# Starting the tiles of the normalized x at multiples of 64 bytes of a partition

## The chip, the core and the metric

The kernel runs on one core of one Trainium2 chip. The metric is the time of one execution on the device in microseconds. The kernel before takes 344.67 us, the median of three runs (344.66 to 345.06).

## What is computed

A block of a transformer with two residual steps, for 2 sequences of 512 tokens with 1,024 features each. First, the layer-normalized x and a context are rounded to 8 bits, centred and multiplied; the product is added to x. Then the sum is layer-normalized again and goes through a shared gated MLP (512 hidden columns) and, for each token, two routed experts (256 hidden columns each).

```python
x = x + tanh(g_xattn[0]) * matmul(fake_quant(layernorm(x)), fake_quant(ctx))
xt = layernorm(x)                                  # 1024 tokens x 1024
gate = router(xt)                                  # 2 of 16 experts for a token
for w1, b1, w2, b2, w3, b3, ge in experts:
    h = silu(xt @ w1 + b1) * (xt @ w2 + b2)        # 256 hidden columns
    y = y + ge[:, None] * (h @ w3 + b3)
z = silu(xt @ sw1 + sb1) * (xt @ sw2 + sb2) @ sw3 + sb3    # 512 hidden columns
x = x + tanh(g_ffn[0]) * (y + z)
```

With these inputs only two experts are chosen by any token, so the kernel computes two experts for all 1,024 tokens and weights them by the gates. More experts, or unusual zero points, lead to branches that are not taken here.

## The kernel before

Tokens are handled in 8 tiles of 128 rows, X0 to X7, four for each sequence (batch) b. All float32 products of the MLPs are made from two pieces of each operand, a high part[...] and the low rest: high x high, high x low and low x high, three passes over 8 blocks of 128 features.

The second normalization's result is transposed on TensorE (`px`, L288) and split into a high tile XH and a low tile XL for each batch. `xh` (L145, mostly on ScalarE) copies the high part out of PSUM; `xl` (L298, VectorE) writes the rest. Each of the four tiles is 128 partitions x 8 blocks x 512 tokens of float32, 16,384 bytes of a partition. They are the moving operand of every up-projection, with the weights (in slabs) as the stationary one:

- L476 (`um`) and L327 (`up_mm`), 256 tokens wide: the first units of the shared MLP, 288 and 96 matmuls.
- L327 (`up_mm`), 512 tokens wide: the rest of the shared MLP (192 matmuls in bank tiles named sp), expert 0 (192, e0p) and expert 1 (192, e1p).

GpSimd also adds XH and XL to one float32 tile xf for the router (L557). In the down-projections (`down`, L372, L373, L375, and `down_last`, L360 to L362, for the last tile) the hidden values are the stationary operand, and the moving one is a slab of weights, 512 columns wide (256 in the last two pieces of the last tile): 192 matmuls for the shared MLP, 96 for expert 0, and 84 + 6 of 512 columns and 12 of 256 for expert 1. The names are spo, e0po and e1po for the outputs, sd, e0d and e1d for the weights, sh, e0h and e1h for the hidden values; h or l at the end is the high or low part.

The tiles of batch 1 share their places with the attention. Slot `xh1` first holds qT of each batch in turn (the quantized x, transposed, bf16, stationary) and then XH1; slot `xl1` first holds cq (the quantized context, bf16, moving) and then XL1. The attention's matmuls are at L233.

The first part, up to about 95 us, is a list of steps written out by hand (START); behind it the program's order holds. All loads and stores are started by SyncE's queue.

SBUF is laid out by pools, in the order in which they are opened: const, keep, small, route, slabs (22 buffers of 4,096 bytes). A slot begins at a multiple of 32 bytes. In the built program of the kernel before, the tiles begin at these bytes of a partition:

| tile or pool | first byte | modulo 64 |
|---|---|---|
| X0 to X7, 4,096 each (pool keep) | 21664 | 32 |
| XH0 | 54432 | 32 |
| XL0 | 70816 | 32 |
| slot xh1: qT, then XH1 | 87200 | 32 |
| slot xl1: cq, then XL1 | 103584 | 32 |
| pool small | 119968 | 32 |
| first slab | 138240 | 0 |
| end of the last slab | 228352 | 0 |

Every block of XH or XL is 2,048 bytes long and every slab 4,096, so all blocks of a tile have the tile's place modulo 64.[...]

Of the kernel before, what the change touches and what calls it, by code (L numbers as in the profile page):

```python
# [10 lines left out]
F32R = mybir.dt.float32r  # L11
BF16 = mybir.dt.bfloat16
# [6 lines left out]
P = 128  # L19
D = 1024  # L20
KD = D // P
B = 2
S = 512
TB = S // P
# [7 lines left out]
SC = 2 * INTER // P  # L32
EPS = 1e-5
LOWEST = -3.4028234663852886e38

# the order in which the start's loads and steps are issued, each step as function.arguments
LOADS = "x.1 x.3 c.0 c.1 x.2 c.2 c.3 c.4 c.5 c.6 c.7.0 c.7.1 w.1.1 x.4 b w.1.0 w.0.1 x.5 w.0.0"
# [40 lines left out]
def flamingo_block(  # L78
# [5 lines left out]
    of = out.rearrange("b s d -> (b s) d")  # L84

    const = ctx.enter_context(tc.tile_pool(name="const", bufs=1))
    keep = ctx.enter_context(tc.tile_pool(name="keep", bufs=1))
# [14 lines left out]

# [1 line left out]
    sc_in = const.tile([P, 6], F32, name="sc_in")  # L104
    nc.sync.dma_start(sc_in, scal.partition_broadcast(P))

# [1 line left out]
    X = [keep.tile([P, D], F32, name=f"X{t}") for t in range(NT)]  # L108

    # the engine that starts the DMAs; the paths that are rarely taken use GpSimd's queue  # L110
    dq = [nc.sync]
# [5 lines left out]

# [1 line left out]
    mhalf = const.tile([P, 1], F32, name="mhalf")  # L119
# [12 lines left out]
    nc.vector.tensor_scalar(nz, sc_in[:, 0:4], -1.0, None, ALU.mult)  # L132
    # zero points that bf16 holds exactly, less any quantized value, are integers of 0..255
    z8 = const.tile([P, 4], U8, name="z8")
# [20 lines left out]
    H = D // 2  # L155
    half = lambda h: ts(h, H)
# [3 lines left out]

# [1 line left out]
    def bn(t, h):  # L162
# [8 lines left out]
    def qa(t, eng):  # L171
        rb = [small.tile([P, 1], F32, name=f"{n}{t}", tag=n, bufs=4) for n in ("r", "qa", "qb")]
        ab_[t] = rb
        pick(eng).tensor_scalar(rb[0], mv_[t][:, 1:2], EPS, None, ALU.add)

# [36 lines left out]

# [1 line left out]
    c8_, raws, qT, cq, acc = {}, {}, {}, {}, {}  # L214
# [21 lines left out]

# [1 line left out]
    sq_, md_, xn_, px_ = {}, {}, {}, {}  # L238

    def e(t, h):  # L240
        """The residual and its sum."""
        if h == 0:
            sq_[t] = [small.tile([P, 2], F32, name=f"{n}{t}", tag=n, bufs=4) for n in "sq"]
        xs = X[t][:, half(h)]
        nc.vector.scalar_tensor_tensor(  # L245
            xs, acc[t][h], cx_scale, xs, ALU.mult, ALU.add, accum_out=sq_[t][0][:, h : h + 1]
        )

    def sq(t, h):
        """H^2 times the squared deviations from the mean of half a row, H values."""  # L250
        if h == 0:
            xn_[t] = slab(f"xn{t}", F32)
        s, q = sq_[t]
        nc.scalar.activation(  # L254
            xn_[t][:, half(h)], X[t][:, half(h)], AF.Square,
            bias=s[:, h : h + 1], scale=-float(H), accum_out=q[:, h : h + 1],
        )

    def fm(t, eng):
        """The mean, and what the difference of the halves' means adds to the variance."""  # L260
        s, eng = sq_[t][0], pick(eng)
        d = small.tile([P, 1], F32, name=f"d{t}", tag="d", bufs=4)
        eng.tensor_tensor(d, s[:, 0:1], s[:, 1:2], ALU.subtract)
        eng.tensor_scalar(d, d, d, H / 2.0, ALU.mult, ALU.mult)
        nm = small.tile([P, 1], F32, name=f"nm{t}", tag="nm", bufs=4)
        eng.tensor_scalar(nm, s[:, 0:1], s[:, 1:2], -1.0 / D, ALU.add, ALU.mult)
        md_[t] = nm, d

    def fc(t, eng):
        d = md_[t][1]  # L270
        pick(eng).tensor_scalar(d, sq_[t][1][:, 0:1], d, EPS * D * H * H, ALU.add, ALU.add)

# [33 lines left out]

# [1 line left out]
    def load_up(name, w1, w2, c):  # L308
# [44 lines left out]
    def down_last(name, t, hid, w3, scale):  # L353
        """A tile in column pieces, each stored as soon as it is done."""
        n = len(hid)
        for lo, w in ((0, 512), (512, 256), (768, 256)):
            cols = slice(lo, lo + w)
            po = bank(f"{name}po{t}_{lo}")[:, :w]
            for c, ((hh, hl), (wh, wl)) in enumerate(zip(hid, w3)):
                nc.tensor.matmul(po, hh[:, ts(t, P)], wh[:, cols], start=c == 0, stop=False)  # L360
                nc.tensor.matmul(po, hh[:, ts(t, P)], wl[:, cols], start=False, stop=False)
                nc.tensor.matmul(po, hl[:, ts(t, P)], wh[:, cols], start=False, stop=c == n - 1)  # L362
            nc.vector.scalar_tensor_tensor(X[t][:, cols], po, scale, X[t][:, cols], ALU.mult, ALU.add)
            dq[0].dma_start(of[ts(t, P), cols], X[t][:, cols])
# [22 lines left out]

    # ================= program =================
    XH, XL = ([keep.tile([P, KD, S], F32R, name=n), None] for n in ("XH0", "XL0"))
    sw1c = lambda c: sw1[:, ts(c, P)].rearrange("(k p) n -> p k n", p=P)  # L390
# [21 lines left out]
    for load in LOADS.split():  # L412
        kind, *at = load.split(".")
        at = [int(a) for a in at]
# [15 lines left out]

# [1 line left out]
    bT = const.tile([P, NB], F32, name="bT")  # L432
# [5 lines left out]

    # TensorE's clock is low until it has been busy for a few microseconds
    zero = const.tile([P, S], BF16, name="zero")  # L440
# [8 lines left out]

    # biases of the hidden layers, as columns  # L450
    def pb():
# [5 lines left out]

    # shared weights, split: half h of the rows of matrix i, hidden columns c
    def wh(c, i, h, eng):
# [8 lines left out]

    # hidden columns c of tokens lo..lo+255: matrix i, pass p of three
    def um(c, lo, i, p):  # L470
# [38 lines left out]

    # router weights, padded to the columns of a quarter of TensorE, and constants of the router  # L510
    rwf = const.tile([P, KD, QC], F32, name="rwf")
# [5 lines left out]
    lowest = const.tile([P, NT * E], F32, name="lowest")  # L517
# [9 lines left out]
    def stage(b):  # L527
        """The buffers of a batch's attention."""
        qT[b] = keep.tile([P, TB, KD, P], BF16, name=f"qT{b}", tag="xh1")
        cq[b] = keep.tile([P, KD, D], BF16, name=f"cq{b}", tag="xl1")  # L530

    def xx():
        XH[1], XL[1] = (keep.tile([P, KD, S], F32R, name=n, tag=n.lower()) for n in ("XH1", "XL1"))

# [8 lines left out]

# [1 line left out]
    def rt(name, shape=(P, NT, E), dtype=F32):  # L545
# [6 lines left out]
    def router_x(b):  # L552
        """The normalized x, transposed, in one float32 piece."""
        xs = []
        for i in range(4):
            x = slab(f"xf{b}_{i}", F32, (P, 2, S))
            nc.gpsimd.tensor_tensor(  # L557
                x, XH[b][:, ts(i, 2)].bitcast(F32), XL[b][:, ts(i, 2)].bitcast(F32), ALU.add
            )
            xs.append(x)  # L560
        return xs

    # the four quarters of TensorE's columns work at the same time, each on a fourth of the rows of D
    def router_logits(b, lT, xs):
# [19 lines left out]
    def first_max(name, v, n):  # L584
        """One-hot of the first largest of the last n."""
        m = rt(f"{name}m", (P, NT))
        nc.vector.tensor_reduce(m, v, AX.X, ALU.max)
        o = rt(f"{name}o", (P, NT, n))
        nc.vector.tensor_tensor(o, v, over(m, n), ALU.is_equal)
        order = tie[:, E - n :].unsqueeze(1).to_broadcast([P, NT, n])  # L590
        nc.vector.tensor_mul(o, o, order)
        nc.vector.tensor_reduce(m, o, AX.X, ALU.max)
        nc.vector.tensor_tensor(o, order, over(m, n), ALU.is_equal)
        return o

    # of all experts some token chose: 16 - e; of the others: 0
    key = route.tile([P, E], F32, name="key")
# [48 lines left out]
    def next_expert(j):  # L646
        """Of the chosen experts left, the one of lowest index: its index, gates and hidden biases."""
        m = rt(f"m{j}", (P, 1))
# [19 lines left out]

# [1 line left out]
    def expert(j, e, gv, bv, store):  # L670
# [32 lines left out]

    # the rest of the shared MLP's hidden layer, with the router in between
    lT = slab("lT", F32)
# [17 lines left out]
    chosen = [next_expert(j) for j in range(2)]  # L723
# [3 lines left out]

# [1 line left out]
    def attention_exact(b):  # L729
# [64 lines left out]

# [1 line left out]
    n_exp = nc.values_load(n_chosen[0:1, 0:1], min_val=2, max_val=E)  # L796
# [54 lines left out]
```

## Time and profile before

| | |
|---|---|
| median of three timed runs | 344.67 us |
| span of the profiled execution, first to last instruction | 342.9 us |
| what the timed median has beyond that span | 1.8 us |
| TensorE matmuls | busy 321.7 us, 94% of the span |
| VectorE / ScalarE / GpSimd | busy 57% / 28% / 23% |
| TensorE's granted clock, mean | 0.989 |
| DMA traffic | 31.45 MB, mean 92 GB/s |

The profile gives the profiled execution's time as its span; what the device adds before the first and after the last instruction is the third row, taken from the timed runs. A matmul's duration in the profile contains its way through the array, which overlaps with the next one's. How many matmuls fit into a stretch of time is read from their starts, and that pace is what counts in a stream of them.

### The profile page before, as it was taken

The page shows a single profiled execution, that of the slowest core. Times are in us where ns is not written, and L with a number is a line of the kernel's source. Part 1 is how long each engine was busy: PE and PEld are TensorE (multiplying, and loading weights), DVE is VectorE, ACT ScalarE, POOL GpSimd, SP SyncE. Part 2 cuts the span into 40 slices and gives each one's busy share as a digit, 9 for nine tenths or more (in the row PEclk, how much of TensorE's full clock was granted, in tenths as well). Part 3 has the DMA queues.
Part 4 walks back from the last instruction along what each step waited for, and adds up shares of the span by engine and source line. Part 5 has one row for each costly group of instructions (what it writes and reads, how often), then busy time and mean ns, then how long its engine had stood idle before and what let it go on. Part 6 is the DMA issues. An engine that isn't in the chain of part 4 may idle for free.

```text
span 342.9 us, 4322 instructions
## 1 busy us (share of the span) xinstructions
PE 321.7 (94%) x1673; PEld 254.5 (74%) x1673; DVE 197.0 (57%) x335; ACT 95.4 (28%) x148; POOL 79.0 (23%) x110
## 2 busy tenths in 40 slices
PE   6588899989999999999999999999999999999990
PEld 2244886769998686888888888888888888888870
DVE  3879999879723126736754632494484135834560
ACT  2756877672213135120200002112400012030000
POOL 2795798868600740000000000000000000000000
PEclk9899999999999999999999999999999999999997
DMA  6999920000004033101200091201310400001542
GB/s 207 420 375 391 399 62 0 2 0 2 0 2 123 9 118 122 63 0 59 66 0 0 8 329 33 62 2 32 90 61 2 122 0 2 0 0 50 198 183 74
DMA packets 25892, 31.45 MB, mean 92 GB/s; under 512 B 2492, under 2 KB 19204, under 8 KB 25860
## 3 DMA queue, kind: packets, MB, share of 16 engines
q1 hardware_dynamic: 25860, 31.05, 26.5%
q8 instruction: 17, 0.28, 0.3%
q14 instruction: 15, 0.12, 0.1%
HBM read 26.85 MB, written 4.19 MB: 91 GB/s over the span
## 4 chain that ended last, share of the span: by engine, by line
PE 75%; DVE 8%; POOL 5%; ACT 4%; issue 3%; DMA 2%; SPq 0%; DVEq 0%; POOLq 0%
PE sp L327 16%; PE e1p L327 13%; PE e0p L327 13%; PE sp L476 5%; PE spo L373 4%; PE spo L372 4%; PE spo L375 4%; ACT xn L254 2%; PE e0po L372 2%; PE e0po L373 2%; PE e0po L375 2%; PE e1po L373 2%; PE e1po L372 2%; PE e1po L375 2%; DVE xn L283 2%
## 5 line engine op out<-in xcount | busy, mean ns | idle before, releaser
L233 PE MATMUL at<-cq,qT 128*128 128x512 bf16 x128 | 30.3, 379 | 2.5 <-POOL cq L153 1.5
L557 POOL TENSOR_TENSOR xf<-XH,XL 128x1024 f32<-128x1024 f32 x8 | 19.9, 2497 | 22.4 <-PE sp L327 19.6
L233 PEld LDWEIGHTS <-qT 128*128 128x128 bf16 x128 | 12.1, 98 | 15.5 <-issue 2.9
L378 DVE SCALAR_TENSOR_TENSOR X<-spo,tg,X 128x512 f32<-128x512 f32 x16 | 11.3, 746 | 16.0 <-PE spo L375 16.0
L338 DVE SCALAR_TENSOR_TENSOR ssa<-sp,bT,ssa 128x512 f32<-128x512 f32 (+1 forms) x6 | 4.0, 662 | 26.1 <-PE sp L327 26.1
L337 ACT ACTIVATE e0sa<-e0p,bv 128x512 f32<-128x512 f32 x4 | 2.8, 690 | 49.4 <-PE e0p L327 49.4
L378 DVE SCALAR_TENSOR_TENSOR X<-e0po,gv,X 128x512 f32<-128x512 f32 x16 | 11.3, 747 | 7.3 <-PE e0po L375 7.3
L283 DVE TENSOR_SCALAR xn<-X,nm,d 128x512 f32<-128x512 f32 x16 | 13.8, 891 | 1.4 <-POOL d L279 1.3
L378 DVE SCALAR_TENSOR_TENSOR X<-e1po,gv,X 128x512 f32<-128x512 f32 x14 | 9.9, 747 | 8.2 <-PE e1po L375 8.2
L288 PE MATMUL px<-ident,xn 128*128 128x128 f32 x64 | 9.3, 275 | 3.5 <-DVE xn L283 2.3
L337 ACT ACTIVATE e1sa<-e1p,bv 128x512 f32<-128x512 f32 x4 | 2.8, 690 | 34.9 <-PE e1p L327 34.9
L338 DVE SCALAR_TENSOR_TENSOR e1sa<-e1p,bv,e1sa 128x512 f32<-128x512 f32 x4 | 3.0, 752 | 15.9 <-PE e1p L327 15.9
L254 ACT ACTIVATE xn<-X,s 128x512 f32<-128x512 f32 x16 | 11.4, 716 | 1.9 <-DVE X L245 1.4
L245 DVE SCALAR_TENSOR_TENSOR X<-at,cx_scale,X 128x512 f32<-128x512 f32 x16 | 11.6, 742 | 0.1
L165 DVE BATCH_NORM_STATS2 st<-X 128x6 f32<-128x512 f32 x16 | 10.3, 680 | 2.2 <-DMA X<-in_dram 2.2
L338 DVE SCALAR_TENSOR_TENSOR e0sa<-e0p,bv,e0sa 128x512 f32<-128x512 f32 x4 | 3.0, 751 | 14.6 <-PE e0p L327 14.6
L288 PEld LDWEIGHTS px<-ident,xn 128*128 128x128 f32 x64 | 7.2, 141 | 5.6 <-ACT XH L145 2.6
L298 DVE TENSOR_TENSOR XL<-px,XH 128x512 fp32r<-128x512 f32 x16 | 10.4, 679 | 0.8 <-ACT XH L145 0.8
L386 DVE SCALAR_TENSOR_TENSOR X<-sbias,tg,X 128x1024 f32<-128x1024 f32 x8 | 10.3, 1284 | 0.3
L153 POOL TENSOR_SCALAR cq<-q8c,nz 128x1024 bf16<-128x1024 uint8 (+1 forms) x8 | 10.0, 1250 | 1.0 <-DVE q8c L223 0.6
L208 PE MATMUL pq<-ident_b,qx 128*128 128x128 bf16 x64 | 5.4, 228 | 4.7 <-ACT qx L151 4.4
L386 DVE SCALAR_TENSOR_TENSOR X<-e1bias,gv,X 128x1024 f32<-128x1024 f32 x8 | 9.8, 1280 | 0.0
(402 smaller groups left out, 830.9 us busy)
## 6 DMA issues: line engine op xcount, KB each, us to landing
cr<-in_dram SPq DMA_DIRECT2D x15, 512.0 KB, 9.2
out_dram<-X SPq DMA_DIRECT2D x15, 256.0 KB, 2.4
X<-in_dram SPq DMA_DIRECT2D x7, 512.0 KB, 9.0
X<-in_dram SPq DMA_DIRECT2D x2, 256.0 KB, 4.1
cr<-in_dram SPq DMA_DIRECT2D x2, 256.0 KB, 9.1
sb1r<-in_dram SPq DMA_DIRECT2D x1, 512.0 KB, 9.0
sa1r<-in_dram SPq DMA_DIRECT2D x1, 512.0 KB, 7.2
sb0r<-in_dram SPq DMA_DIRECT2D x1, 512.0 KB, 8.2
```

Source lines behind the costliest of these rows:

```text
L233: nc.tensor.matmul(acc[t][h], qT[b][:, t % TB, k, :], cq[b][:, k, half(h)], start=(k == 0), stop=(k == KD - 1))
L254: nc.scalar.activation(xn_[t][:, half(h)], X[t][:, half(h)], AF.Square, bias=s[:, h : h + 1], scale=-float(H), accum_out=q[:, h : h + 1],)
L283: nc.vector.tensor_scalar(xn_[t][:, half(h)], X[t][:, half(h)], nm, r, ALU.add, ALU.mult)
L288: nc.tensor.transpose(px_[t, q][:, k, :], xn_[t][:, ts(4 * q + k, P)], ident)
L327: nc.tensor.matmul(p, wx[:, k, :], xx[b][:, k, cols], start=first and k == 0, stop=last and k == KD - 1)
L372: nc.tensor.matmul(po[h], hh[:, ts(t, P)], wh[:, ts(h, 512)], start=first, stop=False)
L373: nc.tensor.matmul(po[h], hh[:, ts(t, P)], wl[:, ts(h, 512)], start=False, stop=False)
L375: nc.tensor.matmul(po[h], hl[:, ts(t, P)], wh[:, ts(h, 512)], start=False, stop=last)
L378: nc.vector.scalar_tensor_tensor(xs, po[h], scale, xs, ALU.mult, ALU.add)
L386: nc.vector.scalar_tensor_tensor(X[t], bb, scale, X[t], ALU.mult, ALU.add)
L476: nc.tensor.matmul(up_[c, lo, i], w[:, k, :], x[0][:, k, lo : lo + 256], start=p == 0 and k == 0, stop=p == 2 and k == KD - 1,)
L557: nc.gpsimd.tensor_tensor(x, XH[b][:, ts(i, 2)].bitcast(F32), XL[b][:, ts(i, 2)].bitcast(F32), ALU.add)
```

## The change

The four tiles XH0, XL0, XH1 and XL1, and qT and cq that share slots with the latter two, are asked for with an alignment of 64 bytes. All tiles of one slot ask for the same. Comments and docstrings go too, and two empty lines take the place of comments; no instruction is added, removed or put elsewhere.

```diff
 EPS = 1e-5
+
+LINE = 64
 LOWEST = -3.4028234663852886e38
...
-    XH, XL = ([keep.tile([P, KD, S], F32R, name=n), None] for n in ("XH0", "XL0"))
+    XH, XL = ([keep.tile([P, KD, S], F32R, name=n, align_bytes=LINE), None] for n in ("XH0", "XL0"))
...
     def stage(b):
-        """The buffers of a batch's attention."""
-        qT[b] = keep.tile([P, TB, KD, P], BF16, name=f"qT{b}", tag="xh1")
-        cq[b] = keep.tile([P, KD, D], BF16, name=f"cq{b}", tag="xl1")
+
+        qT[b] = keep.tile([P, TB, KD, P], BF16, name=f"qT{b}", tag="xh1", align_bytes=LINE)
+        cq[b] = keep.tile([P, KD, D], BF16, name=f"cq{b}", tag="xl1", align_bytes=LINE)
 
     def xx():
-        XH[1], XL[1] = (keep.tile([P, KD, S], F32R, name=n, tag=n.lower()) for n in ("XH1", "XL1"))
+        XH[1], XL[1] = (keep.tile([P, KD, S], F32R, name=n, tag=n.lower(), align_bytes=LINE) for n in ("XH1", "XL1"))
```

By the tile library's description, a pool that is asked for an alignment begins the slots of that tag on it wherever the pool's base is, and reserves the alignment less 32 bytes for each such tag. With four tags that is 4 x 32 = 128 bytes. Worked out from the table above: X0 to X7 stay; XH0 begins at 54464, XL0 at 70848, slot xh1 at 87296, slot xl1 at 103680, all multiples of 64; the pool small begins at 120096 and the first slab at 138368, each 128 further and at the same place modulo 64.

## The prediction, made before the change was run

> **What bounds the kernel now.** I read the page first (section 1, then the chain), then the groups by form on TensorE, then the chain in order of time, and last the timeline where a pace can be read from starts.
>
> ```profile
> span 342.9 us, 4322 instructions
> PE 321.7 (94%) x1673; PEld 254.5 (74%) x1673; DVE 197.0 (57%) x335; ACT 95.4 (28%) x148; POOL 79.0 (23%) x110
> PE 75%; DVE 8%; POOL 5%; ACT 4%; issue 3%; DMA 2%; SPq 0%; DVEq 0%; POOLq 0%
> ```
>
> TensorE is busy for 94% of the span and is 75% of the chain that ended last. Busy is not yet bound, so the chain's order matters more:
>
> ```profile
> 95.05 22.64 PE sp L327 x144
> 117.68 1.85 PE pl L568 x16
> 119.54 11.44 PE sp L327 x48
> 130.98 1.85 PE pl L568 x16
> 132.83 0.59 PE plt L578 x4
> 133.42 0.47 PE sp L327 x2
> 134.33 22.02 PE sp L327 x94
> ...
> 200.13 44.98 PE e0p L327 x192
> 245.10 0.23 PE e0po L372
> ...
> 266.87 44.98 PE e1p L327 x192
> 311.85 0.23 PE e1po L372
> ```
>
> From 95 us to about 333.7 us nothing but matmuls stands on the chain. In that stretch a nanosecond per matmul is a nanosecond of the kernel, times their number. The paces follow from the starts: an up-projection stage of an expert is 44.98 us for 192 matmuls, 234.3 ns each. The down-projection between them, from 245.10 to 266.87, is 21.77 us for 96 (eight tiles of 12), 226.8 ns each. Both stream 512 float32 columns and load 128x128 float32 weights before each one. Their durations show the same step:
>
> ```profile
> L373 PE MATMUL e0po<-e0d0l,e0h0h 128*128 128x512 f32 x16 | 6.2, 389 | 0.0
> L327 PE MATMUL e0p<-XH,e0a0h 128*128 128x512 f32 x16 | 4.1, 396 | 0.0
> L327 PE MATMUL e0p<-XL,e0b1h 128*128 128x512 f32 x16 | 4.1, 396 | 0.0
> ```
>
> Every 512-wide group that streams XH or XL stands at 396 or 397 ns apart from two that begin a stage (407 and 409); every one that streams a slab (sd, e0d, e1d) stands at 389 or 390 (395 for the first of all). By the memory map of the kernel before, XH and XL begin 32 bytes past a multiple of 64 and the slabs begin on one. That is the one fact that lines up with the change.
>
> **The change part by part.**
>
> *Addresses.* Nothing is removed, added or moved in any engine's order or in SP's or POOL's queue; there is no new wait. Only addresses differ: XH0, XL0 and the two shared slots go from 32 to 0 modulo 64. What lies behind `keep` moves too. The pool reserves 32 bytes for each of the four aligned tags, 128 in all, so `small`, `route` and the slabs move by 128 and keep their place modulo 64. It still fits: the slabs end at 228,480 of 229,376 bytes.
>
> *512-wide up-projections.* They are 192 in the shared MLP (48 for c=1, 48 for c=2, 96 for c=3) and 192 in each expert: 576. The nearest row for "the same matmul from a tile on a multiple of 64" is the down-projection, 226.8 ns. 576 x (234.3 - 226.8) = 4.3 us, all on the chain. Bounds: nothing, if the 7.5 ns has another cause; and 576 x (234.3 - 217) = 10 us, if alignment also took away what the float32 stream pays over the bf16 one. That stream is in the trace too:
>
> ```profile
> 69.63 1.03 PE L233 MATMUL at<-cq,qT 128*128 128x512 bf16 x4
> ```
>
> Four matmuls take 1.03 us including the last one's 379 ns, so three starts are 0.65 us apart, 217 ns each. I take 226.8, because the slabs have the alignment and still stand there. Here the Trainium skill speaks twice. TensorE: Matmul & The Clock Gate, section "Back-to-back issue gap", has N/2.4 + 2.5 ns, 215.8 at N = 512, and its account of a matmul's steps says that weights come over a read port of their own and take nothing from the stream. The bf16 row agrees; the float32 rows, at 226.8 and 234.3 with a weight load beside each, do not. By the rule the sum would be 576 x 18.5 = 10.7 us; by the rows it is 4.3, and I follow the rows. SBUF — State Buffer, section "Specifications (TRN2)", speaks against the change: its cachelines have 16 bytes. A tile 32 bytes past a multiple of 64 starts on such a line already, and 2,048 bytes of a row cover 128 lines either way. By that rule the change is worth nothing and the time stays at 344.7. The two paces stand against it, but they don't show that the address is what parts them; that is the largest doubt here, and it is rival 1.
>
> *256-wide up-projections.* 288 at L476 and 96 at L327. Their pace is 0.95 us for 8 in the rows below, 119 ns; the nearest aligned row is the end of the last tile, whose starts at 332.33, 332.45 and 332.57 are 120 ns apart.
>
> ```profile
> 94.88 1.11 PE L327 MATMUL sp<-XH,sa0h 128*128 128x256 f32 x8
> 95.83 1.11 PE L327 MATMUL sp<-XL,sa0h 128*128 128x256 f32 x8
> ...
> 332.33 0.28 PE L362 MATMUL e1po<-e1d0h,e1h0l 128*128 128x256 f32 x1
> 332.45 0.28 PE L360 MATMUL e1po<-e1d1h,e1h1h 128*128 128x256 f32 x1
> 332.57 0.28 PE L361 MATMUL e1po<-e1d1l,e1h1h 128*128 128x256 f32 x1
> ```
>
> So here alignment buys nothing, and may cost 1.2 ns each: 0.5 us if all 384 were on the chain. About 230 are (all 96 at L327, and at L476 17% of the chain's first 95 us, some 135), so I take 0.3 us. Bounds: 0.5 us lost; or 0.7 us gained, if they came to 116 ns, the lowest spacing among them (230 x 3 ns).
>
> *Attention and other engines.* cq lies off 64 before, and its bf16 stream already runs at 217 ns: nothing. The writes of XH and XL (L145, L298) and POOL's sum of the two (L557, 2497 ns each) keep their sizes. In the first 95 us some writes are on the chain ("DVE XL L298" is 3.4% of it, 3.2 us). No row shows an aligned twin, so 5% either way is 0.2 us, and I take zero. POOL's sums run beside matmuls; if that cover were gone, 5% of 19.9 us is 1 us.
>
> *What is late next.* With up-projections 3% shorter, the weights of the following stage must still be split in time. The timeline has the low part of e1's first down weights made by DVE from 303.10 for 1.23 us, used from 311.9; e0a1's low part ends at 215.1, used at 226.2. Each is ready 7 us or more ahead, against 1.4 us that a stage loses, and their own releases move forward with TensorE. The routing result that pcn (L637) waits for is ready at 146.8, 9 us ahead. Nothing takes the place of the time saved. The tail behind the last matmul (add, store, 9.2 us) is unchanged.
>
> *Sum.* -4.3 + 0.3 = -4.0 us against the profiled execution's span of 342.9 us: 338.9. The median of the timed runs, 344.67, stands 1.8 us above that span; what lies around it does not change, so 344.67 - 4.0 = 340.6 us. By its own bounds this case runs from 339.7 (4.3 and 0.7 gained) to 340.9 (4.3 gained, 0.5 lost), and with 0.2 us for the writes from 339.5 to 341.1.
>
> **The rivals.**
>
> *1. Another cause, or a larger boundary; no change.* Up and down streams differ in more than the address: up takes a new stationary tile for each matmul where down loads one for several, and up writes 24 times into one bank where down alternates. Against the bank: the last tile's 512-wide pieces (L360 to L362) write one bank six times in a row at 227 ns. Against the weights: the step between two hidden blocks in the down stream changes them at no extra time. And slabs are at multiples of 1,024, so the rows can't say that 64 is enough. The 256-wide rows, with no gain from alignment, speak for this rival. Time: 344.7, within 0.5. It also covers a request that moves no tile.
>
> *2. The boundary is 128 bytes; half the gain.* By the arithmetic of the map XH0 and XL0 land 64 past a multiple of 128, and XH1 and XL1 on one. Then only batch 1 speeds up: 48 + 48 + 48 + 96 + 96 = 336 matmuls x 7.5 = 2.5 us, so 342.2.
>
> *3. The slabs go off 64; slower.* If the pool grew by 32 bytes and not 128, every slab would begin 32 past a multiple of 64: the weights of all up-projections, and both operands of the down ones. If a matmul is slow as soon as either operand is off, up stays at 234.3 and the 378 + 6 512-wide down-projections rise from 226.8 to it: 2.9 us, 347.5. It decides from the point where the reserve is an odd multiple of 32 and the weights' place counts; if only the stream's place counts, this layout still gains 4.3 - 2.9 = 1.4 us. Against it stands the pool's own description, 32 per tag.
>
> **How the numbers follow.** The forecast has 0.66, rival 1 0.16, rival 2 0.09, rival 3 0.09. About 0.2% (0.7 us) is what a measurement of this kernel can tell from no change. Faster: 0.66 + 0.09 = 0.75. Same: 0.16. Slower: 0.09. The predicted time is the likeliest case's 340.6 us. Forecast and rival 2 together hold 0.75, so the range has to reach rival 1 as well: from 339.5 to 344.9.
>
> **What would show it.** In the profile after: the 512-wide groups on XH and XL at 389 ns in place of 396; "PE e0p" and "PE e1p" x192 at 43.5 us in place of 44.98; the first e1po at about 307.8 in place of 311.85; the down-projections still 226.8 ns apart; attention at 217. Rival 2 shows as two values, 396 for batch 0 and 389 for batch 1. Rival 3 shows as 396 on the slabs. The forecast is wrong if the XH groups keep 396, or if a wait appears on TensorE behind 95 us.

## The result: faster by 0.5%, about half of the forecast or less

The changed kernel takes 343.04 us (median of 13 runs) beside 345.0 us for the kernel before; the ratio is 0.9952, with a 95% interval from 0.9938 to 0.9965. By the ratio that is 1.65 us of 345 (1.2 to 2.1 by its interval); the two medians are 1.96 us apart. The forecast was 4.0 us. Its profiled execution has a span of 340.8 us, 2.1 us less than before, and took 342.48 us.

The chain of waits of the kernel after, in order of time (start, length, engine, tile, line; all line numbers of `up_mm` and what follows are two higher than before):

```profile
37.35 7.55 PE sp L478 x64
...
94.84 22.54 PE sp L329 x144
117.39 1.85 PE pl L570 x16
119.24 11.35 PE sp L329 x48
...
133.94 21.70 PE sp L329 x94
...
199.43 44.31 PE e0p L329 x192
243.74 0.23 PE e0po L374
...
265.55 44.31 PE e1p L329 x192
309.86 0.23 PE e1po L374
```

From 95 us on the chain has the same pieces in the same order, still matmuls only. An expert's up-projection stage takes 44.31 us in place of 44.98: 230.8 ns for each matmul, not 226.8. The down-projections between them stand where they stood: 243.74 to 265.55 is 21.81 us. Two stages of experts give 0.67 us each, the last of the shared MLP 0.3, and its other two 0.2. The chain also stands 0.2 us earlier at 95 us, but that is not the streams' doing. In the kernel before, its first piece on XH or XL began at 37.56 us:

```profile
37.56 7.61 PE sp L476 x64
```

The kernel after has it at 37.35, so the 0.2 us were there already, and from this piece to the one at 95 us both kernels take 57.49 us.

The timeline of TensorE shows what 230.8 is made of. Its rows are start, time to the end of the last matmul, and how many; the three ahead of the dots are of batch 0, the four behind them of batch 1:

```profile
199.26 2.01 PE L329 MATMUL e0p<-XH,e0a0h 128*128 128x512 f32 x8
201.11 2.00 PE L329 MATMUL e0p<-XL,e0a0h 128*128 128x512 f32 x8
202.94 1.99 PE L329 MATMUL e0p<-XH,e0a0l 128*128 128x512 f32 x8
...
210.27 2.02 PE L329 MATMUL e0p<-XH,e0a0h 128*128 128x512 f32 x8
212.13 2.03 PE L329 MATMUL e0p<-XL,e0a0h 128*128 128x512 f32 x8
213.99 2.02 PE L329 MATMUL e0p<-XH,e0a0l 128*128 128x512 f32 x8
215.85 2.02 PE L329 MATMUL e0p<-XH,e0b0h 128*128 128x512 f32 x8
```

From 201.11 to 202.94 is 1.83 us for eight, 229 ns each, for batch 0. From 212.13 to 215.85 is 3.72 us for sixteen, 232.5 ns each, for batch 1. All four tiles now begin on a multiple of 64, and yet there are two paces, and neither is the 226.8 ns of the down-projections. 240 matmuls of batch 0 at 5.3 ns less and 336 of batch 1 at 1.8 ns less make 1.9 us: that is the change's gain. The granted clock is 1.00 from 95 to 333 us in both traces, so it does not part the paces.

### The profile page after: what moved, and what is told of

Same layout as the page of the kernel before. It is cut to its first block, busy times and chain, and to the rows that moved or that the text cites. A ratio compares the mean times of both kernels' runs of the same rounds, so it can differ in the third digit from the quotient of the medians.

```text
span 340.8 us, 4322 instructions
## 1 busy us (share of the span) xinstructions
PE 320.7 (94%) x1673; PEld 254.5 (75%) x1673; DVE 197.1 (58%) x335; ACT 95.3 (28%) x148; POOL 79.2 (23%) x110
## 4 chain that ended last, share of the span: by engine, by line
PE 75%; DVE 8%; POOL 5%; ACT 4%; issue 3%; DMA 2%; SPq 0%; DVEq 0%; POOLq 0%
PE sp L329 16%; PE e0p L329 13%; PE e1p L329 13%; PE sp L478 5%; PE spo L374 4%; PE spo L375 4%; PE spo L377 4%; ACT xn L256 2%; PE e0po L374 2%; PE e0po L375 2%; PE e0po L377 2%; PE e1po L377 2%; PE e1po L374 2%; PE e1po L375 2%; DVE xn L285 2%
## 5 line engine op out<-in xcount | busy, mean ns | idle before, releaser
L235 PE MATMUL at<-cq,qT 128*128 128x512 bf16 x128 | 31.4, 391 | 1.6 <-POOL cq L155 1.3
L147 ACT CAST XH<-px 128x512 fp32r<-128x512 f32 x13 | 7.2, 585 | 9.4 <-PE px L290 9.4
L388 DVE SCALAR_TENSOR_TENSOR X<-e0bias,gv,X 128x1024 f32<-128x1024 f32 x8 | 9.8, 1277 | 0.0
```

Source lines behind the costliest of these rows:

```text
L235: nc.tensor.matmul(acc[t][h], qT[b][:, t % TB, k, :], cq[b][:, k, half(h)], start=(k == 0), stop=(k == KD - 1))
L388: nc.vector.scalar_tensor_tensor(X[t], bb, scale, X[t], ALU.mult, ALU.add)
```

## The experiments

After the result I looked for what else differs between the two batches, and between up and down. Theory: it is not where the moving tile begins, but how far it begins from the stationary one, modulo 256 (what is left when multiples of 256 bytes are taken away). The kernel before has 54432 - 138240, which is 160 modulo 256, for every up-projection. The kernel after has 54464 - 138368, 64, for batch 0, and 87296 - 138368, 128, for batch 1. In the down-projections both operands are slabs: 0. The rivals are the theory of the prediction (multiples of 64) and absolute places without any relation.

**m1_offsets: the streams by themselves.** A kernel of matmul streams only, in float32r, the type of XH, XL and the split weights in the slabs. The two operands are slices whose first byte is chosen:

```python
nc.tensor.matmul(
    b, W[:, s // 4 + k * P : s // 4 + k * P + P], M[:, m // 4 + k * S : m // 4 + k * S + S],
    start=i == 0, stop=i == n - 1,
)
```

> This kernel leaves the whole block out: it copies x to the output and between that runs 56 streams of 40 float32r matmuls (128x128 stationary, 512 columns moving, a new stationary tile and a new moving row for every matmul, as in the up-projections), each from its own first byte of the moving tile (m) and of the stationary tile (s) past a multiple of 1024. Stream names give m and s in bytes, digits as letters a=0 to j=9. In the two kernels a duration stands about 162 ns above the pace, so 389 ns means 227 and 396 to 397 means 234. Theory of the prediction (the moving tile's place modulo 64 sets the pace): every stream with m a multiple of 64 at 389 ns, every stream with m at 32 modulo 64 at 396 to 397, whatever s is. Rival (the distance m - s counts, since the kernel before had 160 and 234.3 ns, the kernel after 64 for batch 0 and 229, 128 for batch 1 and 232.4, and the down-projections 0 and 226.7): streams of equal m - s stand alike for every s; m - s = 0 at 389 ns also where both are at 32; 64 at 391, 128 at 395, 160 at 397. Rival (only the absolute places count, no relation): rows of one m alike over s, but not ordered by multiples of 64.

The timeline of TensorE in this kernel; the distance between two starts, by 40, is the pace. First m = 32, 64, 96, 128 and 160 with s = 0, and the stream behind them for the last one's end:

```profile
29.60 9.50 PE L97 MATMUL madc_saaa<-M,W 128*128 128x512 f32 x40
38.94 9.33 PE L97 MATMUL mage_saaa<-M,W 128*128 128x512 f32 x40
48.10 9.49 PE L97 MATMUL majg_saaa<-M,W 128*128 128x512 f32 x40
57.43 9.49 PE L97 MATMUL mbci_saaa<-M,W 128*128 128x512 f32 x40
66.76 9.53 PE L97 MATMUL mbga_saaa<-M,W 128*128 128x512 f32 x40
76.13 9.49 PE L97 MATMUL mbjc_saaa<-M,W 128*128 128x512 f32 x40
```

These are 233.5, 229.0, 233.3, 233.3 and 234.3 ns. Now s = 32, with m = 32, 64, 96, 160 and 192 (distances 0, 32, 64, 128, 160):

```profile
215.08 9.28 PE L97 MATMUL madc_sadc<-M,W 128*128 128x512 f32 x40
224.20 9.50 PE L97 MATMUL mage_sadc<-M,W 128*128 128x512 f32 x40
233.54 9.33 PE L97 MATMUL majg_sadc<-M,W 128*128 128x512 f32 x40
242.70 9.45 PE L97 MATMUL mbga_sadc<-M,W 128*128 128x512 f32 x40
251.99 9.53 PE L97 MATMUL mbjc_sadc<-M,W 128*128 128x512 f32 x40
261.35 9.24 PE L97 MATMUL mcii_sadc<-M,W 128*128 128x512 f32 x40
```

228.0 (with its first few matmuls; 226.7 once they have passed), 233.5, 229.0, 232.3 and 234.0. Both operands 32 bytes off a multiple of 64 run as fast as any; a moving tile on a multiple of 64 beside weights at 32 runs at 233.5. Over the late matmuls of each stream, the same distances gave the same paces at s = 64, 128, 160 and 256, to 0.3 ns but for distance 128, which stood at 233.2 for s = 0 and at 232.3 otherwise. At s = 0 these late paces are:

| distance, bytes | 0 | 32 | 64 | 96 | 128 | 160 | 192 | 224 | 256 |
|---|---|---|---|---|---|---|---|---|---|
| ns from start to start | 226.7 | 233.3 | 229.0 | 233.4 | 233.2 | 234.3 | 233.3 | 233.3 | 226.7 |

From 256 to 512 the row repeats. So the paces of the 512-wide streams in both kernels are all found by the distance alone: 160 (234.3 measured there), 64 (229), 128 (232.5), 0 (226.8). The theory of the prediction falls, and so does that of absolute places.

**r_slabs160: the kernel before, with nothing aligned.** XH and XL stay 32 past a multiple of 64; the slabs follow them there.

```diff
     # of all experts some token chose: 16 - e; of the others: 0
+    route.tile([P, 40], F32, name="gap_r")
```

> The kernel before with 160 unused bytes in the pool route, so that every slab moves by 160 bytes: XH, XL (untouched) and the slabs all lie 160 past a multiple of 256, that is 32 past a multiple of 64, and the distance of moving and stationary tiles is 0 modulo 256. Distance theory: up-projections at 226.7 ns like the down-projections, 576 x 7.6 = 4.4 us less, ratio 0.987. Theory of the prediction (multiples of 64 of the moving tile): up stays at 234.3, down rises to it, 2.9 us more, ratio 1.008.

Measured: 340.41 us beside 344.86, ratio 0.9872 (0.9844 to 0.9900). From the groups by form and from the chain of this kernel:

```profile
L372 PE MATMUL e0po<-e0d0h,e0h0h 128*128 128x512 f32 x16 | 6.2, 389 | 0.0
L327 PE MATMUL e0p<-XH,e0a0h 128*128 128x512 f32 x16 | 4.0, 389 | 0.0
L327 PE MATMUL e0p<-XL,e0b1h 128*128 128x512 f32 x16 | 4.0, 389 | 0.0
```

```profile
198.63 43.52 PE e0p L327 x192
242.15 0.23 PE e0po L372
```

43.52 us for 192 is 226.7 ns: the whole forecast gain, in a layout in which not one of these tiles begins on a multiple of 64.

**r_both0: distance 0, on multiples of 256.**

```diff
+    keep.tile([P, 24], F32, name="gap")
     XH, XL = ([keep.tile([P, KD, S], F32R, name=n), None] for n in ("XH0", "XL0"))
...
     # of all experts some token chose: 16 - e; of the others: 0
+    route.tile([P, 40], F32, name="gap_r")
```

> The kernel before with 96 unused bytes ahead of XH0 and 160 in the pool route: XH, XL and the slabs all on multiples of 256, distance 0. Both theories: up at 226.7 ns, 4.4 us less, ratio 0.987. If the one before this stands here too, 64 bytes are not what counts.

Measured: 341.02 us, ratio 0.9879 (0.9853 to 0.9904); the two expert stages take 43.52 us each, as in r_slabs160. Where the tiles lie in absolute terms has no part in it that these runs could tell.

**r_dist64: both batches at distance 64.** The same edit with 160 bytes ahead of XH0 and 96 in `route`.

> The kernel before with 160 unused bytes ahead of XH0 and 96 in the pool route: XH and XL of both batches at 64 modulo 256, the slabs on multiples of 256. Distance theory: 229.0 ns for both batches (in the changed kernel only batch 0 had this distance), 576 x 5.3 = 3.1 us less, ratio 0.991, e0p x192 at 43.97 us. Theory of the prediction: 226.7 ns, ratio 0.987. If batch 1 was slow for what lies beside it and not for its address: batch 1 stays at 232.4, ratio 0.995.

Measured: 341.46 us, ratio 0.9902 (0.9878 to 0.9927). The chain:

```profile
199.13 43.96 PE e0p L327 x192
...
264.90 43.96 PE e1p L327 x192
```

229.0 ns over all 192. Batch 1, 232.5 ns in the changed kernel, follows its distance.

**r_mult64_dist160: multiples of 64 at the old distance.** Only `keep.tile([P, 8], F32, name="gap")` ahead of XH0: XH and XL begin on multiples of 64, the slabs 32 past one.

> The kernel before with 32 unused bytes ahead of XH0, nothing else: XH and XL come onto multiples of 64 as in the changed kernel, and the slabs, 32 further as well, stay at the old distance of 160. Distance theory: up at 234.6 ns, down at 226.7, ratio 1.000. Theory of the prediction: up at 226.7 (4.4 us less); the down-projections, whose tiles are now off 64, at 226.7 or at 234.3 (2.9 us more): ratio 0.987 or 0.996.

Measured: 344.71 us, ratio 0.9998 (0.9982 to 1.0014). The chain and the groups:

```profile
199.90 44.97 PE e0p L327 x192
244.87 0.23 PE e0po L372
```

```profile
L372 PE MATMUL e0po<-e0d0h,e0h0h 128*128 128x512 f32 x16 | 6.2, 389 | 0.0
L327 PE MATMUL e0p<-XH,e0a0h 128*128 128x512 f32 x16 | 4.1, 396 | 0.0
```

The alignment that the change asks for is there and buys nothing. The down-projections, all off 64 now, stay at 389. This is also the layout of the prediction's rival 3, and it is not slower.

**m2_widths: what the steps depend on.** Streams as in m1_offsets, with other widths, another type and narrower weights.

> Leaves the whole block out, like m1_offsets. Streams named m and a distance in letters (a=0 to j=9): float32r, 512 columns, every 8 bytes from 0 to 256; w_m: 256 columns, every 32 bytes; bf_m: bfloat16 for both operands, 512 columns, every 32 bytes; lc_m: float32r with 64 stationary columns in place of 128; th_m: float32r with 384 columns. Theory now (reads of the weight load and of the stream meet in the memory, and their distance modulo 256 says how often): the pace repeats at 256; bfloat16, whose weight load is over sooner, at 216 to 217 for every distance; with 64 weight columns the share over 216 ns (10.9 at distance 0, 18.4 at 160) falls to about half, 221 and 225; with 384 columns the same nanoseconds[...], so 173 at 0 and 181 at 160; with 256 columns[...], no distance gains as much as 7 ns, and distance 0 stands at 120 as in the kernels with distance 0 (120.6). Rival (a row or line boundary that the stream crosses, with no part of the weight load in it): bfloat16 shows the same steps in places, and 64 weight columns change nothing.

Rows of its timeline; w_ is 256 wide at distances 0, 160 and 192, lc_ has 64 weight columns at 112 and 160, th_ is 384 wide at 0, 64 and 160:

```profile
327.17 7.84 PE L106 MATMUL w_maaa<-Mdt.float32r,Wdt.float32r 128*128 128x256 f32 x64
...
365.19 7.67 PE L106 MATMUL w_mbga<-Mdt.float32r,Wdt.float32r 128*128 128x256 f32 x64
372.70 7.42 PE L106 MATMUL w_mbjc<-Mdt.float32r,Wdt.float32r 128*128 128x256 f32 x64
379.96 7.73 PE L106 MATMUL w_mcce<-Mdt.float32r,Wdt.float32r 128*128 128x256 f32 x64
...
491.25 9.23 PE L106 MATMUL lc_mbbc<-Mdt.float32r,Wdt.float32r 128*64 128x512 f32 x40
500.32 9.50 PE L106 MATMUL lc_mbga<-Mdt.float32r,Wdt.float32r 128*64 128x512 f32 x40
509.66 7.09 PE L106 MATMUL th_maaa<-Mdt.float32r,Wdt.float32r 128*128 128x384 f32 x40
516.59 7.09 PE L106 MATMUL th_mage<-Mdt.float32r,Wdt.float32r 128*128 128x384 f32 x40
523.52 7.10 PE L106 MATMUL th_mbga<-Mdt.float32r,Wdt.float32r 128*128 128x384 f32 x40
```

- bfloat16: 215.8 ns from start to start at all nine distances. No step, as expected.
- 384 columns: 173.3 ns at all three distances; 516.59 - 509.66 is 6.93 us for 40. I had expected 181 at 160.
- 64 weight columns: 233.5 ns at 160 (500.32 to 509.66), not 225; and 230.3 at distance 0, worse than with 128 columns. The fastest of the four distances tried is 112, at 226.8 (491.25 to 500.32). Half the weights did not halve what is lost.
- 256 columns: 120.0 at distance 0, 117.4 at 160, and 113.3 at 192 (once settled; 372.70 to 379.96 is 113.4 for all 64). Distance 0, the best at 512 columns, is one of the two slowest here; 96 has 120.0 too.
- 512 columns every 8 bytes: nothing but 0 and 256 reaches 226.7; the odd multiples of 8 lie between 232.5 and 238.2.

So there is no step of this kind for bfloat16, and the one for float32r depends on the width. The part of the theory that counted reads of the weight load in proportion is not borne out. Three distances did not repeat between the two kernels, with both tiles at the same places: 112 stood at 226.8 in m1_offsets and at 231.1 here, 48 at 233.3 and at 230.0, and 128 at 233.2 and at 232.4. What came before them in the list of streams was different; whether that is the reason was not tried.

**r_dist192 and r_dist192_256: can the 256-wide pace be used?** The first moves XH and XL to 192. The second also makes each 512-wide up-projection as two of 256 columns:

```diff
-            for wx, xx, first, last in ((wh, XH, True, False), (wh, XL, False, False), (wl, XH, False, True)):
...
+            for q in range(0, n, 256):
+                for wx, xx, first, last in ((wh, XH, True, False), (wh, XL, False, False), (wl, XH, False, True)):
+                    for k in range(KD):
+                        nc.tensor.matmul(
+                            p[:, q : q + 256], wx[:, k, :], xx[b][:, k, lo + q : lo + q + 256],
...
```

> The kernel before with 32 unused bytes ahead of XH0 and 224 in the pool route: XH and XL at 192 modulo 256, slabs on multiples of 256, distance 192; XH and XL on multiples of 64. By the streams measured alone: 512-wide up-projections at 233.3 ns (576 x 1.0 = 0.6 us less than before), 256-wide ones at 113.3 ns in place of 119 (1.3 us less for the 230 or so on the chain): ratio 0.9945. If a place on a multiple of 64 counted by itself: 512-wide at 226.7, ratio 0.983.

> As r_dist192, and every 512-wide up-projection is made as two of 256 columns, 1152 matmuls in place of 576, with twice the weight loads; the down-projections stay 512 wide. By the streams measured alone: 113.3 ns each, 226.6 for two, so 4.4 us less than before there and 1.3 us less in the 256-wide units: 5.7 us, ratio 0.9835, under the best so far (0.987). Rival: at 256 columns the weight loads bound the stream in the kernel and writes of other engines disturb it, 119 ns each: 1152 x 119 - 576 x 234.3 = 2.1 us more, less 1.3: ratio 1.002.

Measured: r_dist192 343.89 us beside 345.13, ratio 0.9960 (0.9939 to 0.9981), its expert stages 44.80 us for 192, 233.3 ns, as the stream had it. Its 256-wide units on the timeline:

```profile
94.06 1.07 PE L327 MATMUL sp<-XH,sa0h 128*128 128x256 f32 x8
94.96 1.07 PE L327 MATMUL sp<-XL,sa0h 128*128 128x256 f32 x8
95.87 1.07 PE L327 MATMUL sp<-XH,sa0l 128*128 128x256 f32 x8
```

94.06 to 95.87 is 1.81 us for 16, 113 ns each, where before had 119. (The units that ran ahead of 76 us in this kernel, at the same distance, settled at 118.) Again XH and XL lie on multiples of 64, and the 512-wide pace is 233.3. r_dist192_256 came out at 343.02, ratio 0.9936 (0.9911 to 0.9960), which neither expectation had: its last stage of the shared MLP ran at 113.9 ns, but the expert stages did not:

```profile
197.40 45.23 PE e0p L328 x384
```

That is 117.8 ns for each at the same distance. Why a stream settles at 113 in one stage and at 118 in another is open. The fastest versions stay r_slabs160 and r_both0, which these intervals don't tell apart; both lie wholly under the changed kernel's 0.9938 to 0.9965.

## Why the prediction was wrong

- *The bound.* Right: the chain from 95 us is matmuls, and the nanoseconds saved per matmul arrived in the time: 1.9 us by the paces, 1.65 by the ratio. No wait appeared, and nothing else became late.
- *The addresses.* The tiles came to the bytes that were worked out, and the slabs kept their place modulo 64.
- *The 512-wide up-projections: the step that failed.* I took the down-projection as "the same matmul from a tile on a multiple of 64" and 226.8 ns as the pace to reach. The two differ in the place of the moving tile, and also in its distance to the weights: 160 for up, 0 for down. I compared what is common to all moving tiles of a group and not the pair of operands of one matmul. The change moved the distance to 64 and 128, so the term of 4.3 us measured 1.9. r_slabs160 gives the 4.4 us without the alignment, and r_mult64_dist160 the alignment without a gain. The range was wide enough for 343.04 us only because it reached as far as rival 1; for its own case the prediction had at most 341.1.
- *The rules that I set aside.* The Trainium skill's 16-byte cachelines (SBUF — State Buffer, section "Specifications (TRN2)") would make the alignment worth nothing. For the alignment as such that is what r_mult64_dist160 measured, ratio 0.9998; but places that are all on 16-byte boundaries differ by up to 8 ns by their distance, of which that rule says nothing. The other page's account, that a weight load takes no read bandwidth from the running matmul (TensorE: Matmul & The Clock Gate, section "Step-by-step: what each phase is for"), does not hold as a rule of pace here: moving only the slabs, the weights among them, by 160 bytes took 7.6 ns off every 512-wide float32 up-projection. And I used that page's N/2.4 + 2.5 ns as a rule for streams, where its section "Back-to-back issue gap" gives it for a single matmul and about 131 ns for a stream of weight loads and matmuls at N = 512. No stream of 512 columns here comes near 131: the bfloat16 ones stood at 215.8, with a weight load for each matmul.
- *256-wide units.* 0.3 us lost was expected, and nothing was lost: the units at L329 kept their 119 ns. The row that the term rested on has distance 0, where r_slabs160 gave these units 120.6 ns, but the change brought them to 64 and 128.
- *Attention and the rest.* Right: bfloat16 shows no step at any distance in m2_widths.
- *The rivals.* Rival 1 (another cause) had the cause right in kind, but took it to leave the time alone. Its difference in weight loads does not exist: the profile before has 1,673 weight loads for 1,673 matmuls, so the down-projection loads for each one too. And the rows by which I held the bank and the weights against it are all of down-projections, at distance 0, where the distance could not show. Rival 2 saw that the batches would part, and had the sign wrong: batch 0, off 128, was the faster. Its 342.2 us came nearest to the 343.04 measured, by luck. Rival 3's price did not arise, since the slabs kept their place modulo 64; r_mult64_dist160 moved them off it and showed no price, the distance within the down-projections being 0 wherever the slabs lie.

## What to carry to other kernels

Where a stream of float32 matmuls bounds a kernel, compare the places of the two operands of each matmul with one another, here modulo 256, and not each with a boundary. Two rows of a profile are a fair pair for an address only when everything else that an address decides is the same in both; a few streams with chosen offsets settle it in one run. And any change of a pool's size moves whatever lies behind it: a gap of 160 unused bytes was worth 1.3% of this kernel, ratio 0.9872.

## What the runs showed of the hardware that I had not expected

- The pace of float32r matmuls of 512 columns with a 128x128 weight load each depends on the distance of the two operands' first bytes, modulo 256: from 226.7 ns at 0 to 234.3 at 160 on multiples of 32, and up to 238.2 at 168. Where both lie makes no difference beyond 0.3 ns at distances 0, 32, 64 and 160, at six places of the stationary tile. What in the memory or in TensorE makes it so was not shown.
- The best distance depends on the width: 0 at 512 columns, 192 at 256 (113.3 ns in place of 117 to 120), none at 384 (173.3 at the three distances tried).
- The starts repeat in short patterns, such as 226, 227, 227 at distance 0 and a round of seven between 231 and 238 at 160, and a stream needs some ten matmuls to fall into its pattern. Which one it falls into was not always the same at the same distance: 112 had 226.8 and 231.1, 48 had 233.3 and 230.0, and the 256-wide streams at 192 had 113.3 and 117.8, both within one kernel. So the distance alone does not fix the pace everywhere.
